# RWKV: output, gate and value products in tiles of 128 tokens, with residual rows brought to the tile and back by DMA

## The chip, the cores and the metric

The kernel runs on one core of a Trainium2 chip (trn2). The metric is device time in microseconds (us). The kernel before takes 3527.89 us, the median of three runs (3525.93 to 3533.52). The kernel after was not run before the prediction went on record.

## What is computed

Four layers work on the same residual stream `x` of 16 sequences, 100 tokens each, 512 channels wide, in fp32 (where the code has `...`, the five mixes of `xa` with its predecessor, the products `r`, `k`, `v`, `w`, `g`, and the normalising of the scan's output `og` per head are left out): a cross-attention block, an RWKV block, a cross-attention block with a feed-forward part, and a second RWKV block. The change is in the RWKV block, which runs twice (layers 1 and 3). Cut to what matters:

```python
def _block(x, state, ...):
    xa = _ln(x, ln1_w, ln1_b)
    ...
    s = a + w_t[..., :, None] * s         # the scan over 100 tokens, a = k_t v_t
    ...
    x1 = x + og * g @ Wo.T                # output product
    xc = _ln(x1, ln2_w, ln2_b)
    sx2 = jnp.concatenate([state[:, 0:1] - xc[:, :1], xc[:, :-1] - xc[:, 1:]], axis=1)
    xk2 = xc + sx2 * ffn_maa_k
    xr2 = xc + sx2 * ffn_maa_r
    rr = jax.nn.sigmoid(xr2 @ Wfr.T)      # gate product
    kk = jnp.square(jax.nn.relu(xk2 @ Wfk.T))   # key product
    return x1 + rr * (kk @ Wfv.T)         # value product
```

The output, gate and value products each multiply 1600 rows by a 512 x 512 matrix. What is added to the residual is one row per token.

## The kernel before

**Layout.** The residual lies in SBUF for the whole kernel as 16 tiles `xb[b]` of 100 tokens by 512 channels, one for each sequence (line 196). RWKV works on groups of `G` = 4 sequences, `T` = 400 tokens. Normalised inputs, the gated scan output (`gc`), the channel part's mixes (`xk`, `xr`) and the squared keys (`kk`) lie turned: 128 channels on partitions, four such pieces for the 512, 400 tokens along the free axis. So the output, gate and value products take 100 columns of such a tile (one sequence) as their left side, the weight's 512 columns as their right side, and sum over the four pieces. `chain` (line 778) records such a product: four matmuls into one PSUM bank, as two halves, each of which is an entry of the queue below, and then `read`.

**The scan and what fills it.** `rwkv` (line 636) is one loop over units `u` (lines 1229 to 1285). The scan has 128 units: 16 chunks (group x 128 channels) of eight. In each unit PE spreads the next values over 128 partitions (`spread`), VectorE does one product and two scans (`product`, `scan`), GpSimd one product with the repeated `r`, and PE gathers sums over two units (`gather`). The rest of the layer lies in the list `pieces`: entries with a cost in us, a first unit (`slot`) and a function. Each unit has a budget `due` (line 1276): 2.5 us up to unit 28, 2.95 up to unit 95, 3.9 after it, less what the unit itself puts on PE. Entries are taken in the order of the list while the budget is positive; a chain that is begun is finished before another. The instructions of PE, VectorE, ScalarE and GpSimd are kept in the order in which the program writes them (lines 65 to 79). SP's queue, on which nearly all loads are issued, is filled by the scheduler of the tile framework: DMAs follow in an order that it derives from the program's order and from when their buffers are ready[...].

**What the list holds.** `projections` (line 799) makes a group's inputs to the scan a group ahead. `output(g)` (line 1210) records the four output products of a group after its last chunk is scanned (at units 32, 64, 96 and 128, to be taken seven units later), ahead of everything else in the list; the residual add on VectorE is put off by one unit with `read_later` (line 183). `channels` (line 971) records the channel part of a group, `channel_stream` (line 1072) strings groups 0 to 2 together (recorded at unit 86, to be taken from unit 93 on), and group 3 is recorded at unit 128. Its parts are: the statistics of `xb` on VectorE, `normed` (ScalarE), `turned` (PE transposes, then ScalarE, GpSimd), the key products `keys` (line 1013), the gate products `gates_of(i)` (line 1026; tanh of the result on ScalarE) and the value products `values(i)` (line 1036; two operations on VectorE, the second of which adds to `xb[b]`). One group's stages are laid around the next group's statistics, in this order (lines 1062 to 1080):

```python
"first":  keys(0..3), gates_of(0), values(0)        # then the next group's statistics
"second": gates_of(1), values(1), gates_of(2), gates_of(3)   # then its normed
"third":  values(2)                                 # then its turned
"fourth": values(3)                                 # then its own first
```

In the last layer `values` also writes the sequence to HBM.

**Buffers.** `stage` gives one of six tiles of 128 x 512 (used by normalised rows, gates and the scan's inputs on their way to HBM); the tag `xm` has three buffers of 128 x 4 x 400, for the mixes; `kk` has one of its own. PSUM has three banks (`mm0` to `mm2`) that all these products share in turn; a bank's late reader is called at the latest when the bank comes round again.

**The scan's own DMAs.** `enter`, `repeat` (line 1099) and `gates` (line 1203) bring a chunk's inputs from HBM on SP's queue: for each half chunk twelve DMAs of 100 KB, which repeat `k`, `w` and `r` over the partitions, and for each chunk four of 200 KB.

Of the kernel before, what the change touches and what calls it, by code (L numbers as in the profile page):

```python
# [9 lines left out]
F32 = mybir.dt.float32  # L10
# [7 lines left out]
G = 4  # L18
# [17 lines left out]
def xattn_sequence(ctx: ExitStack, tc: tile.TileContext, d: dict, out: bass.AP):  # L36
# [599 lines left out]
    def rwkv(n, ws, next_weights, last):  # L636
# [6 lines left out]
        with ExitStack() as es:  # L643
# [83 lines left out]

            steps = lambda t: t.rearrange("p (b t) -> p b t", t=L)
            stage = lambda name: two.tile([128, 512], F32, tag="stage", bufs=6, name=name)
            put = {}  # L730
# [47 lines left out]
            def chain(us, slot, tag, before, ps, lhs, rhs, read):  # L778

                bank = []  # L780

                def half(i):
                    if i == 0:
                        for fn in before:
                            fn()
                        bank.append(slots.bank())
                        begun.append(second)
                    else:
                        begun.clear()
                    for c in (2 * i, 2 * i + 1):  # L790
                        mm(out=ps(bank[0]), lhsT=lhs(c), rhs=rhs(c), start=(c == 0), stop=(c == NC - 1))
                    if i:
                        read(bank[0])

                second = lambda: half(1)
                piece(us / 2, lambda: half(0), slot, tag)
                piece(us / 2, second, slot, tag)

            def projections(g, base):
# [171 lines left out]
            def channels(g, slot):  # L971
# [41 lines left out]
                def keys(co):  # L1013
                    def read(ps):
                        if co == 0:
                            st["kk"] = two.tile([128, NC, T], F32, tag="kk", bufs=1, name=f"kk_{nm}")
                        rl = two.tile([128, T], F32, tag="tm", bufs=4, name=f"rl_{nm}_{co}")
# [8 lines left out]
                def gates_of(i):  # L1026
                    def read(ps):
                        st[i] = stage(f"th_{nm}_{i}")[:L, :]
                        scalar.activation(st[i], ps[:L, :], AF.Tanh, scale=0.5)

                    chain(
                        3.45, slot, None, [], lambda ps: ps[:L, :],
                        lambda c: st["xr"][:, c, i * L : (i + 1) * L], lambda c: cm["Wfr"][:, c, :], read,
                    )

                def values(i):
                    b = g * G + i

                    def read(ps):
                        def add():  # L1040
                            th = st[i]
                            vector.scalar_tensor_tensor(th, th, 1.0, ps[:L, :], ALU.add, ALU.mult)
                            vector.scalar_tensor_tensor(xb[b], th, 0.5, xb[b], ALU.mult, ALU.add)
                            if last:
                                nc.sync.dma_start(out=out[b], in_=xb[b])

                        slots.read_later(ps, add)

                    chain(
                        3.45, slot, None, [], lambda ps: ps[:L, :],  # L1050
                        lambda c: st["kk"][:, c, i * L : (i + 1) * L], lambda c: cm["Wfv"][:, c, :], read,
                    )

                def written(fn):
# [11 lines left out]
                    "first": written(lambda: [keys(co) for co in range(NC)] + [gates_of(0), values(0)]),  # L1066
                    "second": written(lambda: [gates_of(1), values(1), gates_of(2), gates_of(3)]),
                    "third": written(lambda: values(2)),
                    "fourth": written(lambda: values(3)),
# [140 lines left out]
            def output(g, slot):  # L1210

                rest, pieces[:] = pieces[:], []
                before = [lambda: [fn() for c in range(NC) for fn in chunks[NC * g + c]["norm"]]]
                for i in range(G):
                    x = xb[g * G + i]

                    def read(ps, x=x):
                        added[g].append(
                            slots.read_later(ps, lambda: vector.tensor_tensor(x, ps[:L, :], x, ALU.add))
                        )  # L1220

                    chain(
                        3.45, slot, ("wo", g), before, lambda ps: ps[:L, :],
                        lambda c, i=i: chunks[NC * g + c]["g"][:, i * L : (i + 1) * L],
                        lambda c: ws["Wo"][:, c, :], read,
                    )
                pieces.extend(rest)

            UNITS = 32 * NG
            u, due = -42, 0.0  # L1230
            while u < UNITS + 6 or pieces or slots.due:
# [6 lines left out]
                elif u % 32 == 0 and u > 0:  # L1238
                    if u == UNITS:

                        for i in range(len(pieces) - 4, len(pieces)):
                            pieces[i] = (pieces[i][0], u + 8, *pieces[i][2:])
                        rest = channel_stream([NG - 1], u + 8)
                        pieces[len(pieces) - 4 : len(pieces) - 4] = rest[: G + 1]
                        pieces.extend(rest[G + 1 :])
                    output(g - 1, u + 7)
# [28 lines left out]

                due = min(due, 0.0) + (2.5 if 0 <= u < 29 else 2.95 if u < UNITS - 32 else 3.9)
                due -= 0.45 * (u % 2) + 0.7 * (at in (2, 7)) if unit else 0.0
# [444 lines left out]
```

## Time and profile before

| what | us |
|---|---|
| median of three runs | 3527.89 (3525.93 to 3533.52) |
| the profiled execution | 3530.07, of which its span is 3528.3, at a mean granted TensorE clock of 0.935 |
| layer 0 | 0 to 740 |
| RWKV, layer 1: before the scan, scan, after it | 740 to 857, to 1520, to 1600 |
| layer 2: attention, feed-forward | 1600 to 2290, to 2670 |
| RWKV, layer 3: before the scan, scan, after it | 2670 to 2762, to 3430, to 3528 |

The boundaries are rounded, read from the timeline. In the two scans (1331 us together) TensorE is busy for 1245.6 us, VectorE for 885.6 and GpSimd for 811.6. The products that the change touches are these groups of the profile: `mm<-l_Wo,gc` with 256 rows, and for each layer `mm<-l_Wfr,xr` and `mm<-l_Wfv,kk` with 128 rows each, all of 128 x 100 by 128 x 512.

How to read it: PE is TensorE's matmul side, PEld its weight loads, DVE VectorE, ACT ScalarE, POOL GpSimd, SP the sync engine. A row of a group or of the timeline names the engine, the line of the program, the operation, the tile written and the tiles read, their shapes, and how many instructions it stands for; in brackets stands the idle time before it and who ended it. L82 is the helper that records every matmul in program order, and L77 the one for the other engines, so tiles tell operations apart. `SPq` is SP's queue. A layer's number follows the tile's name (`xr_1b`, `kk_3b`).

### The profile page before, as it was taken

What the parts mean: (1) busy time and instruction counts of PE and PEld (TensorE: products, weight loads), DVE (VectorE), ACT (ScalarE), POOL (GpSimd) and SP (SyncE); (2) the same over time, 40 slices, a digit from 0 to 9 for tenths busy, and PEclk for the clock granted to TensorE, in tenths of its full rate; (3) what the DMA queues carried; (4) which work ended last, traced back from release to release, by engine and by line L of the source; (5) the groups of instructions that cost most, each with busy time, mean ns of one, the idle gap of its engine ahead of it and who ended that gap; (6) DMA issues with size and microseconds to landing.
All of it is one profiled execution on the core that took longest, in us unless ns stands there. A gap on an engine that the chain in (4) does not pass through costs nothing. (4 is left out here: it accounts for less than half of the span.)

```text
span 3528.3 us, 46276 instructions
## 1 busy us (share of the span) xinstructions
PE 3217.1 (91%) x17795; PEld 1432.9 (41%) x17795; DVE 1770.8 (50%) x3570; ACT 981.8 (28%) x1715; POOL 1376.4 (39%) x1036
## 2 busy tenths in 40 slices
PE   6899998868999988988999999789998899998898
PEld 3444443333333333334454555345553333333333
DVE  4777777723777665514333333310001477775651
ACT  1322223222233233321322223211112233333232
POOL 1444444443666665511212111210002466665551
PEclk8999999978999989999999999999997899998998
DMA  5000001012434441101000010110012243433310
GB/s 169 21 31 21 31 21 33 1 56 86 126 108 124 126 146 54 38 27 55 25 19 19 19 31 18 39 53 8 10 57 68 87 129 104 134 115 117 87 29 14
DMA packets 153426, 216.60 MB, mean 61 GB/s; under 512 B 23498, under 2 KB 132106, under 8 KB 153206
## 3 DMA queue, kind: packets, MB, share of 16 engines
q1 hardware_dynamic: 130166, 180.87, 17.3%
q10 hardware_dynamic: 23040, 32.78, 2.6%
q8 instruction: 140, 2.29, 0.3%
q14 instruction: 80, 0.66, 0.1%
HBM read 174.25 MB, written 36.04 MB: 60 GB/s over the span
## 5 line engine op out<-in xcount | busy, mean ns | idle before, releaser
L77 POOL TENSOR_TENSOR a<-a,rr 128x800 f32<-128x800 f32 x256 | 480.9, 1879 | 342.4 <-DVE a L77 269.7
L77 DVE TENSOR_TENSOR_SCAN a<-wr,vb 128x400 f32<-128x400 f32 x512 | 475.7, 971 | 19.8 <-PE acc L82 10.9
L77 DVE TENSOR_TENSOR vb<-vb,kr 128x792 f32<-128x792 f32 x256 | 250.5, 979 | 197.0 <-ACT vb L77 195.5
L77 DVE CUSTOM_DVE_ANT_0 junk<-l_sc,mask 100x361 f32<-100x361 f32 x512 | 273.0, 533 | 90.1 <-PE l_sc L82 73.6
L82 PE MATMUL vb<-vc,sel 32*128 32x396 f32 x1024 | 261.0, 568 | 3.4 <-DVE a L77 2.2
L77 DVE TENSOR_TENSOR pt<-l_sc,maskT 121x400 f32<-121x400 f32 x384 | 193.5, 566 | 89.9 <-PE l_sc L82 89.0
L77 ACT ACTIVATE pt<-pt 121x1600 f32<-121x1600 f32 x96 | 147.6, 1538 | 282.2 <-DVE pt L77 280.7
L1425 DVE CUSTOM_DVE_ANT_0 junk<-l2a_sc,mask 100x361 f32<-100x361 f32 x256 | 136.9, 535 | 172.9 <-PE l2a_sc L82 155.7
L77 POOL TENSOR_TENSOR xj<-tm,ext 128x400 f32<-128x400 f32 x160 | 152.8, 962 | 174.3 <-DVE tm L77 168.0
L77 DVE SCALAR_TENSOR_TENSOR tm<-mm,vec,sx 128x400 f32<-128x400 f32 x160 | 99.9, 631 | 235.6 <-PE mm L82 190.9
L1461 POOL TENSOR_TENSOR pa<-pt,pt 121x1600 f32<-121x1600 f32 x16 | 57.2, 3574 | 366.8 <-ACT pt L1456 366.8
L63 PE MATMUL h<-yTb,l_fc 128*128 128x400 f32 x512 | 175.3, 505 | 8.2 <-ACT yTb L229 8.2
L1642 DVE TENSOR_TENSOR x<-pb,x 100x512 f32<-100x512 f32 x16 | 12.8, 799 | 338.3 <-DMA pb<-po 332.7
L82 PE MATMUL v<-l_v_w,ct 128*121 128x512 f32 x384 | 180.0, 613 | 0.0
L82 PE MATMUL k<-ct,l_k_w 128*128 128x361 f32 x512 | 173.0, 481 | 7.3 <-DVE mv_l2a L207 7.3
L77 POOL TENSOR_TENSOR pa<-pt,pt 121x1600 f32<-121x1600 f32 x32 | 114.7, 3586 | 165.5 <-ACT pt L77 165.5
L63 PE MATMUL p<-l_proj,h 128*128 128x512 f32 x384 | 165.4, 592 | 0.0
L77 ACT COPY vb<-s0r 128x8 f32<-128x8 f32 x256 | 43.0, 168 | 408.7 <-PE vb L82 322.9
L82 PE MATMUL l_sc<-kz,qz 32*100 32x361 f32 x1024 | 117.1, 528 | 42.6 <-DVE pt L77 21.7
L82 PEld LDWEIGHTS vb<-vc,sel 32*128 32x128 f32 x1024 | 84.8, 190 | 146.9 <-issue 107.3
L82 PE MATMUL mm<-l_Wo,gc 128*100 128x512 f32 x256 | 124.6, 629 | 8.4 <-POOL gc L77 8.4
L63 PEld LDWEIGHTS h<-yTb,l_fc 128*128 128x128 f32 x512 | 98.1, 192 | 83.3 <-ACT yTb L229 10.1
(258 smaller groups left out, 5305.6 us busy)
## 6 DMA issues: line engine op xcount, KB each, us to landing
kr<-dk SPq DMA_DIRECT2D x256, 100.0 KB
wr<-dw SPq DMA_DIRECT2D x256, 100.0 KB
rr<-dr SPq DMA_DIRECT2D x256, 100.0 KB
ct<-in_ctxT SPq DMA_DIRECT2D x32, 722.0 KB
dk<-k ACTq DMA_DIRECT2D x32, 200.0 KB
kc<-dk SPq DMA_DIRECT2D x32, 200.0 KB
dw<-wd ACTq DMA_DIRECT2D x32, 200.0 KB
dv<-v ACTq DMA_DIRECT2D x32, 200.0 KB
```

The costliest lines, as they stand in the source:

```text
L63: nc.tensor.matmul(out=ps, lhsT=lhs(c), rhs=rhs(c), start=(c == 0), stop=(c == n - 1))
L77: return lambda *args, **kw: tc.keep_in_program_order(op(*args, **kw))
L82: pin(nc.tensor.matmul(**kw))
L1425: nc.vector.tensor_tensor_reduce(out=junk, in0=ss[r][:L, :S2], in1=t["mask"], scale=-1.0, scalar=FLT_MAX, op0=ALU.add, op1=ALU.min, accum_ ...
L1461: nc.gpsimd.tensor_tensor(t["pa"], t["pt"][0], pt, ALU.add)
L1642: nc.vector.tensor_tensor(x, pb[:, i, :], x, ALU.add)
```

## The change

The output, gate and value products no longer go sequence by sequence but in tiles of 128 consecutive tokens of the group: three tiles of 128 and 16 tokens left over. For those 16 the last 32 tokens of the group are taken as the left side, and the 512 output columns are split into four lots of 128, which go into four column groups of 32, so that the result is one 128 x 128 tile: partitions 32r to 32r+31 hold columns 128r to 128r+127 of the last 32 tokens. The first 16 of each 32 are computed twice and not used.

Since a tile of 128 tokens does not match the residual tiles of 100, the residual rows are brought by DMA, SBUF to SBUF, on SP's queue: `rows_in` copies the rows of one or two `xb` tiles into a tile of 128 x 512 (tag `stage`) or, for the left-over, four lots of 32 rows x 128 columns into a tile of the new tag `rest`. VectorE adds there, and `rows_out` copies the rows back. For the output products `rows_in` is issued when the product is begun (`bring`), for the value products when the gate is read. In the last layer the value product's tile goes straight to HBM. Other parts: `kk` takes one of the three `xm` buffers in place of its own; `values(2)` moves from "third" to "second" and `gates_of(3)` from "second" to "third"; the budget is 2.88 in place of 2.95 up to unit 95, 3.5 in place of 3.9 up to unit 127; `output` and the end of the loop are written for either number of entries.

```diff
--- before.py
+++ after.py
@@ -726,6 +726,7 @@
                 scalar.copy(s0r[:, r].rearrange("p c g b -> p (c g b)"), ps[:, : NC * 64])
 
             steps = lambda t: t.rearrange("p (b t) -> p b t", t=L)
+            orow = out.rearrange("b t e -> (b t) e")
             stage = lambda name: two.tile([128, 512], F32, tag="stage", bufs=6, name=name)
             put = {}
             pieces = []
@@ -795,6 +796,59 @@
                 second = lambda: half(1)
                 piece(us / 2, lambda: half(0), slot, tag)
                 piece(us / 2, second, slot, tag)
+            def pieces_of(g, i):
+                for b in range(G):
+                    lo, hi = max(b * L, i * 128), min(b * L + L, i * 128 + 128)
+                    if lo < hi:
+                        rs = slice(lo - b * L, hi - b * L)
+                        yield slice(lo - i * 128, hi - i * 128), xb[g * G + b][rs, :]
+            def rest(g, lo):
+                rs = slice(L - 32 + lo, L)
+                for r in range(4):
+                    ps = slice(32 * r + lo, 32 * r + 32)
+                    yield ps, xb[g * G + G - 1][rs, r * 128 : (r + 1) * 128]
+            def tile_of(nm, i):
+                if i < 3:
+                    return stage(f"{nm}_{i}")
+                return two.tile([128, 128], F32, tag="rest", bufs=3, name=f"{nm}_{i}")
+            def rows_in(nm, g, i):
+                t = tile_of(nm, i)
+                for ps, x in pieces_of(g, i) if i < 3 else rest(g, 0):
+                    nc.sync.dma_start(out=t[ps], in_=x)
+                return t
+            def rows_out(t, g, i):
+                for ps, x in pieces_of(g, i) if i < 3 else rest(g, 16):
+                    nc.sync.dma_start(out=x, in_=t[ps])
+            def row_products(i, slot, tag, before, lhs, rhs, read):
+                if i < 3:
+                    chain(
+                        3.45, slot, tag, before, lambda ps: ps, lambda c: lhs(c)[:, i * 128 : (i + 1) * 128],
+                        rhs, lambda ps: read(ps, ps),
+                    )
+                    return
+                def small():
+                    for fn in before:
+                        fn()
+                    ps = slots.bank()
+                    for c in range(NC):
+                        for r in range(4):
+                            mm(
+                                out=ps[32 * r : 32 * r + 32, :128], lhsT=lhs(c)[:, T - 32 : T],
+                                rhs=rhs(c)[:, r * 128 : (r + 1) * 128], start=(c == 0), stop=(c == NC - 1),
+                            )
+                    read(ps, ps[:, :128])
+                piece(1.0, small, slot, tag)
 
             def projections(g, base):
                 nm = f"{n}_{g}"
@@ -1013,7 +1067,7 @@
                 def keys(co):
                     def read(ps):
                         if co == 0:
-                            st["kk"] = two.tile([128, NC, T], F32, tag="kk", bufs=1, name=f"kk_{nm}")
+                            st["kk"] = two.tile([128, NC, T], F32, tag="xm", bufs=3, name=f"kk_{nm}")
                         rl = two.tile([128, T], F32, tag="tm", bufs=4, name=f"rl_{nm}_{co}")
                         scalar.activation(rl, ps[:, :T], AF.Relu)
                         scalar.activation(st["kk"][:, co, :], rl, AF.Square)
@@ -1024,31 +1078,36 @@
                     )
 
                 def gates_of(i):
-                    def read(ps):
-                        st[i] = stage(f"th_{nm}_{i}")[:L, :]
-                        scalar.activation(st[i], ps[:L, :], AF.Tanh, scale=0.5)
-
-                    chain(
-                        3.45, slot, None, [], lambda ps: ps[:L, :],
-                        lambda c: st["xr"][:, c, i * L : (i + 1) * L], lambda c: cm["Wfr"][:, c, :], read,
+                    def read(ps, got):
+                        st["th", i] = tile_of(f"th_{nm}", i)
+                        scalar.activation(st["th", i], got, AF.Tanh, scale=0.5)
+                        st["x", i] = rows_in(f"cx_{nm}", g, i)
+                    row_products(
+                        i, slot, None, [], lambda c: st["xr"][:, c, :], lambda c: cm["Wfr"][:, c, :], read
                     )
 
                 def values(i):
-                    b = g * G + i
-
-                    def read(ps):
+                    def read(ps, got):
                         def add():
-                            th = st[i]
-                            vector.scalar_tensor_tensor(th, th, 1.0, ps[:L, :], ALU.add, ALU.mult)
-                            vector.scalar_tensor_tensor(xb[b], th, 0.5, xb[b], ALU.mult, ALU.add)
-                            if last:
-                                nc.sync.dma_start(out=out[b], in_=xb[b])
+                            th, x = st["th", i], st["x", i]
+                            vector.scalar_tensor_tensor(th, th, 1.0, got, ALU.add, ALU.mult)
+                            vector.scalar_tensor_tensor(x, th, 0.5, x, ALU.mult, ALU.add)
+                            if not last:
+                                rows_out(x, g, i)
+                            elif i < 3:
+                                nc.sync.dma_start(out=orow[g * T + i * 128 : g * T + (i + 1) * 128], in_=x)
+                            else:
+                                for r in range(4):
+                                    nc.sync.dma_start(
+                                        out=orow[(g + 1) * T - 16 : (g + 1) * T, r * 128 : (r + 1) * 128],
+                                        in_=x[32 * r + 16 : 32 * r + 32],
+                                    )
 
                         slots.read_later(ps, add)
 
-                    chain(
-                        3.45, slot, None, [], lambda ps: ps[:L, :],
-                        lambda c: st["kk"][:, c, i * L : (i + 1) * L], lambda c: cm["Wfv"][:, c, :], read,
+                    row_products(
+                        i, slot, None, [], lambda c: st["kk"][:, c, :], lambda c: cm["Wfv"][:, c, :], read
                     )
 
                 def written(fn):
@@ -1064,8 +1123,8 @@
                     "normed": some(normed, G),
                     "turned": written(lambda: [piece(0.45, lambda c=c: turned(c), slot) for c in range(NC)]),
                     "first": written(lambda: [keys(co) for co in range(NC)] + [gates_of(0), values(0)]),
-                    "second": written(lambda: [gates_of(1), values(1), gates_of(2), gates_of(3)]),
-                    "third": written(lambda: values(2)),
+                    "second": written(lambda: [gates_of(1), values(1), gates_of(2), values(2)]),
+                    "third": written(lambda: gates_of(3)),
                     "fourth": written(lambda: values(3)),
                 }
 
@@ -1209,22 +1268,27 @@
 
             def output(g, slot):
 
-                rest, pieces[:] = pieces[:], []
+                later, pieces[:] = pieces[:], []
                 before = [lambda: [fn() for c in range(NC) for fn in chunks[NC * g + c]["norm"]]]
-                for i in range(G):
-                    x = xb[g * G + i]
-
-                    def read(ps, x=x):
-                        added[g].append(
-                            slots.read_later(ps, lambda: vector.tensor_tensor(x, ps[:L, :], x, ALU.add))
-                        )
-
-                    chain(
-                        3.45, slot, ("wo", g), before, lambda ps: ps[:L, :],
-                        lambda c, i=i: chunks[NC * g + c]["g"][:, i * L : (i + 1) * L],
-                        lambda c: ws["Wo"][:, c, :], read,
-                    )
-                pieces.extend(rest)
+                x = {}
+                def bring(i):
+                    x[i] = rows_in(f"ox_{n}_{g}", g, i)
+                for i in range(4):
+                    def read(ps, got, i=i):
+                        def add():
+                            vector.tensor_tensor(x[i], got, x[i], ALU.add)
+                            rows_out(x[i], g, i)
+                        added[g].append(slots.read_later(ps, add))
+                    row_products(
+                        i, slot, ("wo", g), before + [lambda i=i: bring(i)],
+                        lambda c: chunks[NC * g + c]["g"], lambda c: ws["Wo"][:, c, :], read,
+                    )
+                pieces.extend(later)
 
             UNITS = 32 * NG
             u, due = -42, 0.0
@@ -1238,11 +1302,12 @@
                 elif u % 32 == 0 and u > 0:
                     if u == UNITS:
 
-                        for i in range(len(pieces) - 4, len(pieces)):
+                        kept = max(len(pieces) - 4, 0)
+                        for i in range(kept, len(pieces)):
                             pieces[i] = (pieces[i][0], u + 8, *pieces[i][2:])
-                        rest = channel_stream([NG - 1], u + 8)
-                        pieces[len(pieces) - 4 : len(pieces) - 4] = rest[: G + 1]
-                        pieces.extend(rest[G + 1 :])
+                        own = channel_stream([NG - 1], u + 8)
+                        pieces[kept:kept] = own[: G + 1]
+                        pieces.extend(own[G + 1 :])
                     output(g - 1, u + 7)
                 if u == UNITS - 32 - 3:
                     cm.update(load(n, "Wfk", "Wfr", "Wfv"))
@@ -1273,7 +1338,7 @@
                 if u % 2 and 0 <= (u - 3) // 2 < UNITS // 2:
                     gather((u - 3) // 2)
 
-                due = min(due, 0.0) + (2.5 if 0 <= u < 29 else 2.95 if u < UNITS - 32 else 3.9)
+                due = min(due, 0.0) + (2.5 if 0 <= u < 29 else 2.88 if u < UNITS - 32 else 3.5 if u < UNITS else 3.9)
                 due -= 0.45 * (u % 2) + 0.7 * (at in (2, 7)) if unit else 0.0
                 for p in [p for p in pieces if p[0] == 0 and p[1] <= u]:
                     take(p)
```

## The prediction

> **What bounds the kernel now.** The page's first two parts come first.
>
> ```profile
> span 3528.3 us, 46276 instructions
> PE 3217.1 (91%) x17795; PEld 1432.9 (41%) x17795; DVE 1770.8 (50%) x3570; ACT 981.8 (28%) x1715; POOL 1376.4 (39%) x1036
> ```
>
> TensorE is busy for 91% of the span, VectorE for half. Averages mix stages, so the table by stage comes next (columns: stretch, its length, then busy time of PE, PEld, DVE, ACT, POOL, granted clock, DMA share, GB/s). The first three rows are the scan of layer 1, the fourth its tail.
>
> ```profile
> 857.00:1012.00 155.00, 148.38 (x544) 56.75 (x542) 113.38 (x140) 48.73 (x105) 107.47 (x89) 0.89 0.37 110
> 1012.00:1330.00 318.00, 298.15 (x1140) 113.69 (x1141) 222.19 (x276) 105.98 (x219) 206.04 (x167) 0.93 0.41 122
> 1330.00:1520.00 190.00, 177.76 (x591) 64.14 (x590) 105.84 (x129) 63.85 (x122) 91.72 (x74) 0.94 0.15 43
> 1520.00:1606.00 86.00, 68.11 (x162) 27.93 (x161) 20.70 (x41) 19.98 (x33) 16.90 (x24) 0.87 0.20 66
> ```
>
> In the scan PE is busy 94 to 96% of the time and DVE 56 to 73%. Work taken from PE there is worth nearly its length. What one matmul costs stands in the timeline (start, length, engine, operation):
>
> ```profile
> 1576.40 3.60 PE L82 MATMUL mm<-l_Wfr,xr_1b 128*100 128x512 f32 x8
> 1579.83 3.60 PE L82 MATMUL mm<-l_Wfv,kk_1b 128*100 128x512 f32 x8
> ...
> 2392.18 3.70 PE L1629 MATMUL p<-l_proj,h 128*32 128x128 f32 x128
> 2395.81 1.59 PE L226 MATMUL lnT_l2b<-ident,xn_l2b 100*128 100x100 f32 x16
> ```
>
> The trace has two rows for each fp32 matmul. A chain of four at 512 columns (8 rows) starts 3.43 us before the next. The 592 ns that the groups give for one row is its latency, not its price; the price is 0.43 us. The third line is the same shape of work as the new small piece, in layer 2: 64 matmuls over four column groups take 3.63 us, or 0.057 us each.
>
> [...] four small ones of layer 2 land about 1.9 us after the last issue begins:
>
> ```profile
> 2664.56 2.75 SPq L1636 DMA_DIRECT2D pb<-pr  x4
> ...
> 2668.54 0.69 DVE L1642 TENSOR_TENSOR x<-pb,x 100x512 f32<-100x512 f32 x1 [1.20 <-DMA pb<-pr]
> ```
>
> [...] after the 4.22 us wait below, weight loads stand 0.86 us apart instead of 0.43 for 6 us.
>
> **The change, part by part.**
>
> (a) PE. Each product of a group had four chains, 4 x 3.43. It now has three, and 16 small matmuls: 16 x 0.057 = 0.91. It saves 3.43 - 0.91 = 2.52 us. The layer-2 rows 128*128 128x512 keep the 0.43 us interval, so 128 rows of output cost no more than 100. There are 3 products x 4 groups x 2 layers = 24: 60.5 us at full clock. How much is realised? I set the built order of both kernels out unit by unit (a unit is one product and two scans), with 0.43 and 0.335 us a row for 512 and 400 columns, and DVE at 0.98, 0.93 and 0.58 to 0.69 us. Per layer PE loses 6.4 us in units 29 to 95, 13.0 in 96 to 125, 10.9 in the tail. The sum over units of the larger of PE and DVE falls by 4.8, 10.7 and 10.9: 26.4, or 52.8 for both layers. PE runs ahead of DVE across units, so the truth lies between 52.8 and 60.5: I take 57. The new pacing (2.88 for 2.95, 3.5 for 3.9) leaves each unit's place in the order nearly as it was; it is in this sum.
>
> (b) DVE and ACT do three reads of 128x512 and one of 128x128 for four of 100x512. The reads (0.69 us) do not grow with partitions; the fourth shrinks. 0.45 us each, three adds a product pair, is some 10 us over the kernel, on engines with slack: nothing.
>
> (c) SP issues 10 copies in and 10 out for each output product and each pair of gate and value products (7 out in the last layer's pair): 308 copies, 16 old ones gone. At 0.43 us an issue that is about 125 us on a queue that is idle for most of 3528. Bytes: about 24 MB more, beside 217. Throughput costs nothing; order does. Rows out wait for DVE's add and hold all that SP has behind them, the scan's repeats above all. In the built order those repeats then stand three to four units (14 to 18 us) ahead of need, and take about 9 (twelve issued from 1032.07 on had landed by 1041.44): nothing. Rows in: most tiles have two units (9 us) or more. The exception is the small output tile of groups 0 and 1 (units 45 and 77): it stands behind the tile before it going out, and seven repeats: 0.9 + 3.0 to 4.2 + 1.7 issue + 1.9 landing = 7.5 to 8.7 us, after 4.5 us of a unit. DVE stalls 3 to 4 us; its slack ahead of PE's next spread is about 2 us. 1.5 us x 4 places = 6 us (0 to 12).
>
> (d) Order in the channel part. Before, a whole value chain (3.43) stood between one group's turned rows and the next group's keys; now a small one (0.91). The keys wait for POOL already:
>
> ```profile
> 1395.39 3.29 POOL L77 TENSOR_TENSOR sx_1b<-ext_1b 128x400 f32<-128x400 f32 x4
> ...
> 1401.08 0.94 PE L82 MATMUL mm<-xk_1b,l_Wfk 128*128 128x400 f32 x2 [2.96 <-POOL xk_1b L77]
> ...
> 1475.16 0.94 PE L82 MATMUL mm<-xk_1b,l_Wfk 128*128 128x400 f32 x2 [1.70 <-POOL xk_1b L77]
> ```
>
> The POOL chain is unchanged, so 2.5 us of cover is lost at two groups in each layer: 10 us[...]: 12 (4 to 20).
>
> (e) Tail. The last output product now goes through a copy before its statistics:
>
> ```profile
> 3451.05 14.45 PE L82 MATMUL mm<-l_Wo,gc 128*100 128x512 f32 x26 [4.22 <-POOL gc L77]
> ...
> 3465.34 7.03 PE L82 MATMUL mm<-l_Wfv,kk_3b 128*100 128x512 f32 x16
> ...
> 3471.52 2.93 ACT L77 ACTIVATE xn_3b<-x,shift_3b,rstd_3b 100x512 f32<-100x512 f32 x4 [21.62 <-POOL shift_3b L77]
> ...
> 3472.38 0.30 PE L85 MATMUL mm<-ident,xn_3b 100*128 100x100 f32 x1
> ```
>
> From the end of Wo to the first transpose 7.0 us pass, just hidden by two value chains. Afterwards: add 0.5, four issues 1.7, landing 1.9, one bn_stats and aggregate 0.9, POOL 2.0, ACT 0.8: 7.8 us, covered by one chain and two small ones, 5.2. 2.6 us x 2 layers = 5, and 1 for the clock: 6 (2 to 10).
>
> (f) From layer 1 to 2, layer 2's first context load waits until rwkv's tiles are free (issued at 1598.83, 0.15 us after the last add). Now it waits for the last rows out: +3.6, and the shorter adds give back 0.9: 3 (1 to 5). At the kernel's end the same adds help: -1.
>
> (g) `kk` shares the three `xm` buffers; in the built order each one's last reader on PE precedes its next writer: nothing, unless POOL's mix of the gate input comes early (then in d).
>
> Sum: -57 + 6 + 12 + 6 + 3 - 1 = -31 us. The profiled execution took 3530.07 us, its span plus 1.8; the median is 2.2 lower. 3527.9 - 31 = 3497.
>
> **Rivals.** *Waits cost nothing in the scan* (all 60.5 realised, only e and f left, 9): 3476. For it: PE's 94 to 96%; against it: the POOL wait in d is in the profile. *Gain eaten*: d and e at double, c at its upper end (12 + 40 - 1 + 5 = 56 against 57): about 3527. [...] *Slower, by the rows' round trip*: some 42 row tiles come in during the two scans, on a DMA that is 40% busy. If each stalls DVE by more than its 2 us of slack, PE's spread waits with it. Beyond 31/42 = 0.75 us of PE time a tile the change loses; with rows 5 us behind the repeats (seven of 100 KB, at the 1200 KB in 9.4 us of those twelve, are 5.5 us) half of them would lose 2.5: 42 x 1.2 = 50, less the 31: 3547. Against it: the built order gives most tiles two units. [...]
>
> **Chances.** Forecast 0.60 (own range 3483 to 3512); cheap waits 0.24; gain eaten 0.07; slower 0.09. The range 3473 to 3518 leaves out the slower case, the eaten one and the best end of the cheap one. About 0.2% (7 us) is what a measurement of this kernel can tell from no change: faster by more 0.86, within 0.05, slower 0.09.
>
> **What would show it.** Wo, Wfr and Wfv at 192 rows each over both layers instead of 256, with the small shape beside them; PE's busy time down by about 55; new DVE waits for `ox` of 1 to 4 us at four places; keys waiting 5 us instead of 3 for POOL; a gap of 2 to 3 us before the tail's transposes; the first layer-2 keys 3 us later after the last value product. Wrong: DVE waits for `ox` or `cx` of over 40 us in all, or repeats landing late for POOL.

## The result and the profile after

The changed kernel takes 3519.09 us (median of 8 runs, 3510.95 to 3523.93) against 3529.43 for the kernel before in the same comparison: a ratio of 0.9966, with a 95% interval of 0.9954 to 0.9978. That is 12 us less (8 to 16); forecast were 31, and the range ended at 3518. The profiled execution took 3521.39 us, its span 3519.3. Below, "against before" is always a kernel's ratio to runs of before on the same chip, less 1, times 3528; the 95% intervals reach 3 to 7 us to each side, so a difference between two kernels is good to some 5 to 9 us.

The head of the page after:

```profile
span 3519.3 us, 47909 instructions
PE 3191.7 (91%) x18371; PEld 1448.5 (41%) x18371; DVE 1759.3 (50%) x3570; ACT 978.0 (28%) x1715; POOL 1374.2 (39%) x1036
```

PE's busy time fell by 25.4 us, where 55 were expected. Yet the products are what was forecast. Two groups of matmuls of the kernel after (count, busy us, mean ns, idle time before them):

```profile
L82 PE MATMUL mm<-l_Wo,gc 128*128 128x512 f32 x192 | 96.0, 640 | 8.4 <-POOL gc L77 8.4
...
L82 PE MATMUL mm<-l_Wo,gc 128*32 128x128 f32 x256 | 8.6, 276 | 0.0
```

192 rows in place of 256, and eight small pieces in 8.6 us, 1.1 each. So the work is gone and something else keeps PE "busy". The table by stage shows what: stretches from scan unit to scan unit, first of the kernel before (layer 1: units 29 to 95; units 96 to 126; unit 127 and the tail, up to layer 2's first key matmul; then unit 127 and the tail of layer 3), then of the kernel after. The columns are those of the prediction's table; the number before the last two is the mean granted clock.

```profile
987.25:1313.26 326.01, 302.35 (x1153) 115.39 (x1154) 227.77 (x284) 112.18 (x229) 216.95 (x179) 0.92 0.42 125
1313.26:1499.38 186.12, 173.88 (x593) 63.25 (x593) 110.45 (x133) 64.68 (x127) 98.30 (x79) 0.93 0.18 51
1499.38:1605.80 106.42, 88.53 (x222) 35.27 (x220) 26.02 (x48) 23.57 (x38) 18.77 (x25) 0.89 0.16 53
...
3424.52:3528.30 103.78, 88.88 (x218) 35.03 (x216) 19.53 (x31) 23.58 (x38) 16.44 (x20) 0.90 0.06 16
```

```profile
987.82:1324.81 336.99, 314.10 (x1197) 120.91 (x1198) 227.16 (x284) 107.62 (x222) 210.15 (x172) 0.89 0.43 130
1324.81:1505.32 180.51, 164.16 (x713) 64.96 (x713) 107.83 (x133) 67.42 (x134) 102.88 (x86) 0.92 0.29 85
1505.32:1611.77 106.45, 79.41 (x346) 37.20 (x344) 22.04 (x42) 23.80 (x39) 20.04 (x26) 0.86 0.29 93
...
3423.43:3519.30 95.87, 79.22 (x342) 36.93 (x340) 17.68 (x31) 23.81 (x39) 18.04 (x21) 0.89 0.16 49
```

Units 29 to 95 are 11 us longer, with less to do: PE is busy 12 us more, at a clock of 0.89 in place of 0.92. At half clock the same pair of matmuls is busy for 1.70 us in place of 0.94 (both are shown below), so busy time is not work. The tail has 9 us less of PE time and the same length: 27.0 us without PE in place of 17.9. So three quantities are kept apart from here on, in the profiled execution of each kernel, summed over both RWKV layers from unit 0 to the end of the tail: gaps (length less PE's busy time), the loss to half clock (half of the busy time inside the spells for which the trace's clock records show half the clock), and the work that is left.

| kernel | against before, us | length | gaps | half-clock loss | work |
|---|---|---|---|---|---|
| before | 0 | 1489.9 | 110.0 | 94.1 | 1285.9 |
| e9: before, late budget 3.5 | -37 | 1452.4 | 85.7 | 81.7 | 1284.9 |
| e5: before, both new budgets | -30 | 1463.3 | 79.0 | 87.2 | 1297.1 |
| e11: before, 2.88 and 3.1 | -45 | 1442.7 | 73.4 | 75.1 | 1294.3 |
| e13: changed, old budgets | +8 | 1499.7 | 146.3 | 114.7 | 1238.7 |
| changed | -12 | 1486.9 | 127.0 | 123.8 | 1236.1 |
| e3: output products alone | -13 | 1476.4 | 98.9 | 102.7 | 1274.9 |
| e4: gate and value products alone | -28 | 1465.4 | 108.1 | 99.3 | 1258.1 |
| e2: changed, own rows | -37 | 1450.4 | 116.9 | 95.9 | 1237.7 |
| e7: e2 and a chain as cover | -62 | 1440.6 | 102.7 | 99.8 | 1238.1 |
| e10: e7 with 3.1 | -83 | 1414.0 | 90.6 | 86.4 | 1236.9 |
| e12: e10 with 2.95 | -48 | 1441.2 | 103.9 | 100.6 | 1236.7 |

Work is good to about 12 us: the four kernels with the products of before give 1285 to 1297. The loss to half clock is good to about 7 us a layer: before and e9 run the same program up to unit 95 of each layer, and units 29 to 95 of layer 3 took 325.9 us in one and 332.5 in the other, with gaps of 23.4 and 23.6 and a half-clock loss of 19.0 and 25.9. The profiled executions lie up to 7 us from their kernel's median, so lengths need not differ as the first column does.

Against e5, which has its budgets, the changed kernel has 61.0 us less work, as forecast, and 48.0 us more gaps and 36.6 more half clock.

### The profile page after: what moved, and what is told of

Its sections match the earlier page's. It is cut to its first block, busy times and chain, and to the rows that moved or that the text cites. A ratio compares the mean times of both kernels' runs of the same rounds, so it can differ in the third digit from the quotient of the medians.

```text
span 3519.3 us, 47909 instructions
## 1 busy us (share of the span) xinstructions
PE 3191.7 (91%) x18371; PEld 1448.5 (41%) x18371; DVE 1759.3 (50%) x3570; ACT 978.0 (28%) x1715; POOL 1374.2 (39%) x1036
## 3 DMA queue, kind: packets, MB, share of 16 engines
q1 hardware_dynamic: 148106, 204.35, 19.4%
## 5 line engine op out<-in xcount | busy, mean ns | idle before, releaser
L77 POOL TENSOR_TENSOR pa<-pt,pt 121x1600 f32<-121x1600 f32 x32 | 114.7, 3583 | 165.2 <-ACT pt L77 165.2
L77 POOL TENSOR_TENSOR pa<-pa,pt 119x1600 f32<-119x1600 f32 x32 | 114.4, 3575 | 42.5 <-ACT pt L77 42.3
```

The lines of the kernel that those rows point to most:

```text
L77: return lambda *args, **kw: tc.keep_in_program_order(op(*args, **kw))
```

## The experiments

The theory after the result (A): the left-over output tile stalls VectorE and PE at four places, and half clock follows. Rivals: the gain was lost ahead of the keys (B), or on SP's queue as such (C). This is the place at unit 45 in the kernel after (start, length, engine; SPq is SP's queue):

```profile
1058.24 0.69 DVE L77 TENSOR_TENSOR ox<-mm,ox 128x512 f32<-128x512 f32 x1 [1.85 <-PE mm L82]
...
1058.95 1.66 SPq L828 DMA_DIRECT2D x<-ox  x2
...
1060.65 1.48 SPq L1164 DMA_DIRECT2D wr<-dw  x3
1062.25 1.77 SPq L1164 DMA_DIRECT2D rr<-dr  x4
...
1064.06 2.49 SPq L823 DMA_DIRECT2D ox<-x  x4
...
1067.82 0.29 DVE L77 TENSOR_TENSOR ox<-mm,ox 128x128 f32<-128x128 f32 x1 [6.24 <-DMA ox<-x]
...
1068.26 0.91 PE L82 MATMUL mm<-tz,td_maa_w 64*128 64x400 f32 x2 [2.81 <-DVE ox L77]
...
1078.55 1.70 PE L82 MATMUL mm<-tz,td_maa_w 64*128 64x400 f32 x2
```

SP's queue issues nothing from 1057.48 to 1058.95, until the third tile's add has ended (1058.93). Then the third tile goes out, the seven repeats behind it follow, and the left-over tile comes in, 8.9 us after the third tile's add. VectorE waits 6.2 us, PE 2.8 for a PSUM bank, and then a pair of matmuls takes 1.70 in place of 0.9 us: by the clock records PE is at half clock for 20.5 us here; before, for 6.8.

**e1, the left-over tile first.**

```diff
 def bring(i):
-    x[i] = rows_in(f"ox_{n}_{g}", g, i)
+    for k in {0: (3, 0), 3: ()}.get(i, (i,)):
+        x[k] = rows_in(f"ox_{n}_{g}", g, k)
```

> One edit: the left-over tile's residual rows of each output product are brought when the first tile is begun, before the third tile's rows go back. Theory A (the loss is the round trip of the left-over output tile in groups 0 and 1: VectorE waits 6.3 us at four places, PE then stalls about 3 us and runs some 10 to 14 us longer at half clock, about 9 us a place, 36 in all): VectorE's waits for ox fall from 25 us to under 3, the half-clock spells after units 45 and 77 shrink from 17-20 us to 7, and the time falls by 28 to 36 us, to 3483 to 3491. Theory B (the gain of the small matmuls was never there, or is lost to the key and transpose waits): within 8 us of the changed kernel, 3511 to 3519. Theory C (SP's queue is loaded as such, and the repeats come late): the waits move to other tiles, little is gained, 3505 to 3519.

Measured: 3490.34 us, ratio 0.9898 (0.9882 to 0.9914), 36 us against before and 24 less than the changed kernel. VectorE's waits for ox fell from 25.1 us to none. A holds, B and C fall for this part.

**e2, own rows.** `lots` are three fixed tiles, set to zero once; the sums in the partitions for which no rows are brought are not used.

```diff
-for ps, x in pieces_of(g, i) if i < 3 else rest(g, 0):
+for ps, x in pieces_of(g, i) if i < 3 else rest(g, 16):
...
-return two.tile([128, 128], F32, tag="rest", bufs=3, name=f"{nm}_{i}")
+return next(lots)
```

> One edit: for the left-over tile only the 16 rows that it owns are brought, not the 32 that it computes, so that its way in no longer depends on the third tile's way out; the other partitions hold zeros from the start, and their sums are not used. The order of the program is unchanged. Theory A, if the dependency alone sets the place on the queue: the same as with the tile brought first, 3483 to 3491. If instead the number of copies on the queue counts, as many as before are issued: 3511 to 3519, unchanged.

Measured: 3488.01, ratio 0.9895 (0.9880 to 0.9909). The same as e1 (3490.34), with as many copies as in the changed kernel, and 25 us less than it: the dependency sets the place, not the number of copies. The left-over add now comes early, at unit 45:

```profile
1055.46 0.28 DVE L77 TENSOR_TENSOR rest<-mm,rest 128x128 f32<-128x128 f32 x1
...
1059.34 0.94 PE L82 MATMUL mm<-tz,td_maa_w 64*128 64x400 f32 x2
```

In units 29 to 95 the changed kernel has 5.7 us more gaps and 12.2 more half-clock loss than e2 in layer 1, and 5.3 and 7.2 in layer 3: 11.0 and 19.4 in both. Against e1 it is 11.4 and 14.3. So in both comparisons the half clock costs more than the stall itself.

**e3 and e4, one half of the tiling each.**

```diff
# e3: gates_of, values and their order as before
-row_products(i, slot, None, [], lambda c: st["xr"][:, c, :], lambda c: cm["Wfr"][:, c, :], read)
+chain(3.45, slot, None, [], lambda ps: ps[:L, :], lambda c: st["xr"][:, c, i * L : (i + 1) * L], ...)
# e4: output as before
-row_products(i, slot, ("wo", g), before + [lambda i=i: bring(i)], ...)
+chain(3.45, slot, ("wo", g), before, lambda ps: ps[:L, :], ...)
```

> Only the output products in tiles of 128; gate and value products, and their order, as before; kk in the mixes' buffers and the new budgets stay. Theory A: 8 of the 24 products save 20 us, the four stalls cost 36, the tails 5: slower than before by about 15 to 20 us, 3545. Theory B (loss in the channel part: lost cover ahead of keys): faster than before by 12 to 15, 3515.

> Only the gate and value products in tiles of 128, with their new order, buffers and budgets; the output products as before. Theory A: 16 products save 40 us, the key waits cost some 10, the boundary to layer 2 some 5: faster than before by about 25, 3504. Theory B (the cover lost ahead of the keys eats the gain): within 8 us of before, 3521 to 3529.

Measured: e3 3515.90, ratio 0.9963 (0.9950 to 0.9975); e4 3501.81, ratio 0.9922 (0.9908 to 0.9935). e4 came out where A had it and e3 where B had it, and together they would be 41 us faster where the changed kernel is 12. Neither theory had a place for that, so the question was what both share with the changed kernel: the budgets.

**e5, the budgets alone.**

```diff
-due = min(due, 0.0) + (2.5 if 0 <= u < 29 else 2.95 if u < UNITS - 32 else 3.9)
+due = min(due, 0.0) + (2.5 if 0 <= u < 29 else 2.88 if u < UNITS - 32 else 3.5 if u < UNITS else 3.9)
```

> The kernel before with the new budgets alone (2.88 and 3.5 us a unit). The prediction has them at nothing: 3523 to 3531. Rival: with only the output products tiled, units 96 to 127 got 17 to 19 us shorter in each layer, though one output product lies there; if the budget of 3.5 does that, those units shorten here by 10 or more as well, and what is left over lengthens the tails: 3510 to 3522 if part of it stays.

Measured: 3501.78, ratio 0.9916 (0.9904 to 0.9929), 30 us faster than before, without one tile of 128. So e4's tiles are worth nothing (3501.81 beside 3501.78), e3's cost 17, and the changed kernel's cost 18: A's hit on e4 was chance, and its forecast of e3, 18 slower, holds once e5 is the base. What the budget does shows in units 96 to 126 and in unit 127 with the tail, in layer 1 of e5:

```profile
1310.73:1476.57 165.84, 158.93 (x560) 56.16 (x559) 109.64 (x133) 64.38 (x126) 97.96 (x80) 0.96 0.22 60
1476.57:1591.25 114.68, 100.06 (x257) 41.55 (x258) 26.48 (x49) 28.10 (x47) 26.17 (x32) 0.93 0.15 49
```

The units are 20 us shorter, the tail only 8 longer. With fewer pieces a unit, PE no longer reaches the keys before GpSimd's mixes: the waits of 2.96 and 1.70 us for `xk` and of 4.09 for `rk` are gone, and one of 1.35 for `xk` is left. And the tail has products left to put under its own waits. This is the same e5, ahead of the last output product, where the kernel before waited 4.22 us for `gc`:

```profile
1499.11 1.88 PE L82 MATMUL mm<-l_Wfr,xr_1b 128*100 128x512 f32 x4
1500.83 3.60 PE L82 MATMUL mm<-l_Wfv,kk_1b 128*100 128x512 f32 x8
1504.26 7.03 PE L82 MATMUL mm<-l_Wfr,xr_1b 128*100 128x512 f32 x16
1511.13 13.90 PE L82 MATMUL mm<-l_Wo,gc 128*100 128x512 f32 x32
```

**e6 and e13, the old budgets** in e2 and in the changed kernel (the reverse of e5's diff).

> The left-over tile brings only its own rows, as in e2, and the budgets are those of before. If the budgets are worth nothing: 3484 to 3492, as e2. If the lower budgets carried part of the gain: 3495 or more; if they cost (units 29 to 95 of the channel-only kernel were 3.4 us longer in each layer than before): 3478 to 3483.

> The changed kernel with the budgets of before, nothing else undone: the fourth corner beside before (3527), before with the new budgets (3502) and the changed kernel (3519). If the tiles' loss does not depend on the budget (17 us at the new ones): 3540 to 3550. If the tiles need the lower budget, as own rows did (50 us between the old and the new budgets): 3560 to 3575. The prediction's own step, budgets worth nothing: 3515 to 3523.

Measured: e6 3538.46, ratio 1.0024 (1.0013 to 1.0034); e13 3536.01, ratio 1.0023 (1.0014 to 1.0032). The tiles cost 8 us at the old budgets and 18 at the new ones; the budgets give 30 without tiles and 20 with them. All three guesses for e13 were off, and e6 went far beyond its "3495 or more". Own rows gain nothing at the old budgets (e6 and e13 are equal), because the stall of theory A is not there in e13. At unit 44 the left-over add follows the third tile's at once:

```profile
1056.58 0.69 DVE L77 TENSOR_TENSOR ox<-mm,ox 128x512 f32<-128x512 f32 x1 [1.85 <-PE mm L82]
1057.62 0.29 DVE L77 TENSOR_TENSOR ox<-mm,ox 128x128 f32<-128x128 f32 x1 [0.35 <-PE mm L82]
```

Its rows come in there from 744.6 us on, ahead of the scan, and the third tile's rows go out from 1057.29 on; in the changed kernel the left-over rows come in last (1064.06 after 1058.95, shown above). At the other three places the gap is 0.35 us as well. VectorE does wait 16.1 us for ox in e13, but for three other tiles, those of the third group (units 104 to 107). So the stall belongs to the budget of 2.88 as well as to the dependency.

**e7 and e8, a whole chain as cover ahead of the keys**, e8 with the old budgets.

```diff
-"second": written(lambda: [gates_of(1), values(1), gates_of(2), values(2)]),
-"third": written(lambda: gates_of(3)),
-"fourth": written(lambda: values(3)),
+"second": written(lambda: [gates_of(1), values(1), gates_of(2), gates_of(3)]),
+"third": written(lambda: values(3)),
+"fourth": written(lambda: values(2)),
```

> As e2, and the order in the channel part is gates 1, values 1, gates 2, gates 3, then the small value product, then the next group's transposes, then the value product of the third tile: a whole chain of 3.43 us stands again between the transposes and the keys, where a small one of 0.9 stood. Prediction's step d (2.5 us of cover at two groups in each layer, and some half clock): the key waits fall from 5.3 and 3.9 us back to about 3.0 and 1.7, and 8 to 12 us are gained on e2's 3488: 3476 to 3480. Rival: the wait only moves to the next one for GpSimd (the wait for rk of 4 us that stood there before comes back): 3484 to 3490.

> As e7, with the budgets of before. If both effects are what e6 and e7 show by themselves, they add up: e7's time plus the difference of e6 from e2. If budgets and order work on the same waits, it stands within 4 us of the better one of the two.

Measured: e7 3468.78, ratio 0.9824 (0.9811 to 0.9837), 25 us less than e2 (18 to 32 by the intervals); e8 3512.99, ratio 0.9945 (0.9931 to 0.9959), 28 less than e6. In the changed kernel and in e7 the first of these key waits is:

```profile
1418.75 1.70 PE L82 MATMUL mm<-xk_1b,l_Wfk 128*128 128x400 f32 x2 [5.29 <-POOL xk_1b L77]
...
1482.00 1.63 PE L82 MATMUL mm<-xk_1b,l_Wfk 128*128 128x400 f32 x2 [3.86 <-POOL xk_1b L77]
```

```profile
1389.33 0.94 PE L82 MATMUL mm<-xk_1b,l_Wfk 128*128 128x400 f32 x2 [1.59 <-POOL xk_1b L77]
```

The second wait in e7 is under 1.4 us; in layer 1 of e2, from which e7 starts, PE waits 2.29, 0.53 and 4.53 us at the first of the two and 3.85 at the second. The 4 us wait for `rk` did not come back: layer 1 has a new one of 1.93, layer 3 none. The gain is twice step d's 12, and it adds to the budgets' (25 and 28). Not all of it is cover. The order of e7 also ends the layer with a tile of 128, two copies out, in place of the left-over one, four, and PE waits less ahead of layer 2 (e2, then e7):

```profile
1587.99 0.76 PE L85 MATMUL m8T<-ident,mfr 16*121 16x16 f32 x3 [14.29 <-DMA m<-in_mask]
```

```profile
1576.17 0.75 PE L85 MATMUL m8T<-ident,mfr 16*121 16x16 f32 x3 [9.68 <-DVE mfr L1572]
```

In the profiles units 96 to 126 of the two layers, where the key waits lie, are 15.3 us shorter in e7 than in e2.

**e14, the old order of entries alone** in the changed kernel ("second": gates 1, values 1, gates 2, gates 3; "third": values 2; "fourth": values 3).

> The changed kernel with the order of entries of before: gates 3 ahead of the next group's normed rows, the whole chain of value product 2 ahead of the transposes, the small value product after them. The keys still have only a small product as cover, so step d says nothing changes there: 3515 to 3523. If the move of gates 3 behind the normed rows is what delays GpSimd's mixes: 3500 to 3512.

Measured: 3520.11, ratio 0.9980 (0.9972 to 0.9988), 7 us against before and 5 from the changed kernel; the two intervals overlap. As d says: the small piece, not the moved entries, is what leaves the keys bare.

**e9, e10, e11, e12, one budget each.** 3.5 late with 2.95 early (e9); e7 with 2.88 and 3.1 (e10); before with 2.88 and 3.1 (e11); e10 with 2.95 early (e12). The edits are shown against the line with both new budgets.

```diff
# e10, e11
-3.5 if u < UNITS else 3.9
+3.1 if u < UNITS else 3.9
# e9, e12
-2.88 if u < UNITS - 32
+2.95 if u < UNITS - 32
```

> The kernel before with the later of the two budgets alone: 3.5 us a unit from unit 96 to 127, and 2.95 kept ahead of it. Both budgets together gave 3502. If the later one does it (it removes the key waits of 3.0 and 1.7, the rk wait of 4.1 and the gc wait of 4.2 us from the profile): 3500 to 3510. If the earlier one does (the units before 29 were 4 us shorter in each layer): 3518 to 3527.

> As e7, with 3.1 in place of 3.5 us a unit from unit 96 to 127. Theory D (a budget that is too large for what is left in the list drains the channel part ahead of GpSimd and ScalarE, and leaves the tail no work to put under its waits; tiles take work out of the list, so the budget has to fall with it): the gc wait of 4.2 us at the head of each tail goes, the gaps of units 96 to 127 fall from 12 to under 8 us, and 8 to 18 us are gained: 3451 to 3461. Rival: 3.5 happens to suit one order of pieces, and the waits only move: 3463 to 3478.

> The kernel before with 2.88, and 3.1 us a unit from unit 96 to 127. At 3.5 the profile shows no key wait and no gc wait that a still lower budget could take away, so theory D gives little: 3496 to 3506, within 5 us of the 3502 at 3.5. If a lower budget is good by itself, whatever is in the list: 3485 to 3494.

> As e10, with the earlier budget of before, 2.95 in place of 2.88. In the kernel before, 2.88 cost 12 us (3502 with both new budgets, 3490 with the later one alone), though units 0 to 28 got 4 us shorter in each layer. If that cost belongs to the budget: 3428 to 3436. If it belongs to where that kernel's pieces happen to fall: 3440 to 3452.

Measured: e9 3489.80, ratio 0.9895 (0.9878 to 0.9911); e10 3443.24, 0.9766 (0.9747 to 0.9786); e11 3480.78, 0.9872 (0.9855 to 0.9889); e12 3477.59, 0.9865 (0.9845 to 0.9885). The later budget does it all: 37 us alone. e10 is 83 us faster than before, faster than both kernels of this case. The gc waits at the head of its two tails are gone; in layer 1 products stand there (e10, then the changed kernel's tail in layer 3):

```profile
1489.71 3.60 PE L82 MATMUL mm<-l_Wfv,kk_1b 128*128 128x512 f32 x8
1493.14 3.60 PE L82 MATMUL mm<-l_Wfr,xr_1b 128*128 128x512 f32 x8
1496.58 11.47 PE L82 MATMUL mm<-l_Wo,gc 128*128 128x512 f32 x56
```

```profile
3441.35 2.74 PE L82 MATMUL mm<-l_Wo,gc 128*128 128x512 f32 x6
3448.31 10.62 PE L82 MATMUL mm<-l_Wo,gc 128*128 128x512 f32 x50 [4.22 <-POOL gc L77]
```

Theory D (the budget must fall with the list) is right on the gc wait, and the gain was larger than forecast (20 us on e7); but the gaps of units 96 to 126 fell only from 12.3 and 11.6 us to 10.9 and 8.6, not under 8. And e11 limits it: the kernel before gains another 15 us over e5 from 3.1 as well, in half clock above all (87.2 to 75.1), so a lower budget is good in itself here. With 3.1 the tiles, with own rows and the cover, are at last worth 37 us (e10 against e11). e12 contradicts both its guesses: 2.95 costs 35 us in e10, where in the kernel before it gained 7, about as much as the intervals can tell. The waits ahead of unit 96 do not explain this, since they go with the early budget in both kernels. Here is the one for normed rows in e12 and e9, which have 2.95, then in e10 and e5, which have 2.88:

```profile
1302.52 0.43 PE L85 MATMUL mm<-ident,xn_1b 100*128 100x100 f32 x1 [8.19 <-ACT xn_1b L77]
...
1298.66 0.43 PE L85 MATMUL mm<-ident,xn_1b 100*128 100x100 f32 x1 [8.19 <-ACT xn_1b L77]
```

```profile
1300.80 0.43 PE L85 MATMUL mm<-ident,xn_1b 100*128 100x100 f32 x1 [6.37 <-ACT xn_1b L77]
...
1304.25 0.43 PE L85 MATMUL mm<-ident,xn_1b 100*128 100x100 f32 x1 [6.38 <-ACT xn_1b L77]
```

In both pairs 2.95 adds 14 us of gaps in units 29 to 95 of the two layers. In the kernel before the later stretches make up for it (e9 against e5: 7 us fewer gaps after unit 95, 5.5 less half clock, and 12 less work, which is as far as work is good to); in e12 they do not, and half clock grows by 14.2 as well. Why is not settled.

## Why the prediction was wrong

The direction was right by luck; the size was 12 instead of 31, by two errors of opposite sign and a premise behind both. The tiles and what comes with them cost 18 us (changed kernel against e5), where the prediction had them gain 31; the new budgets, which it had at nothing, gave 30 (e5 against before). The tiles take 60.5 us of work away and still cost 18, so some 79 us were lost, where the prediction allowed 29.5.

- **The premise, "work taken from PE there is worth nearly its length".** It rested on PE's busy share of 94 to 96% in the scan. That share holds half-clock time: 94.1 of 1489.9 us are lost to it before. The sentence on the unit-by-unit sum, with full-clock prices and PE or VectorE as the larger, had no term for either gaps or clock. The work of step a is gone as forecast (61.0 against e5, forecast 60.5 at full clock, of which 57 were to show); it came back as gaps and half clock.
- **Step a, "the new pacing ... leaves each unit's place in the order nearly as it was; it is in this sum".** Wrong, and the largest single term: the budgets alone gave 30 us (e5). I judged places by unit, while what counts is how far the list is drained when GpSimd's mixes are due and when the tail begins.
- **Step c, the left-over output tile, 6 us.** The place and the chain were right. The cost was 25 (e2), for two reasons: VectorE's wait was 6.2 us, not 3 to 4, because only 2.7 us of its unit's work stood between the adds (two scans and a product, 1058.85 to 1061.58), not 4.5; and the half clock after the stall was left out, 19.4 of the 29.2 us that the two layers' units 29 to 95 differ by (14.3 of 24.2 against e1). The number of copies is not the cause: e2 has as many and takes 25 us less. What copies cost in throughput was not measured by itself. The stall also needs the budget of 2.88 (e13), which the step did not see.
- **Step d, 12 us.** The wait came as written, 5 us in place of 3. Giving the cover back gained 25 in all, of which about 5 lie at the boundary to layer 2 and belong to step f. In units 96 to 126 gaps sank by 9.4 us and half clock by 6.5 in e7 against e2. Right mechanism, a cost of about 15 to 20; the half clock, put at 2 by the author's estimate, was mis-sized.
- **Step e, 6 us.** The gap ahead of the tail's transposes was put at 2 to 3 us; the profile after has 3.87 and 3.55. It was costed as the only loss of the tail. Its other one, the 4.22 us wait for `gc`, was there before, and the new budgets alone would have covered it; tiles leave too little in the list to do so.
- **Step f, 3 us.** It was 6.7. The first context load of layer 2 is issued at 1607.42, behind the last rows out, and the keys wait 14.0 us where they waited 7.3 (kernel after; last line: kernel before):

```profile
1602.72 3.39 SPq L828 DMA_DIRECT2D x<-cx_1b  x5
1607.42 0.37 SPq L1389 DMA_DIRECT2D ct<-in_ctxT  x1
...
1611.77 1.54 PE L82 MATMUL k<-ct,l_k_w 128*128 128x361 f32 x2 [13.98 <-DMA ct<-in_ctxT]
```

```profile
1605.80 1.54 PE L82 MATMUL k<-ct,l_k_w 128*128 128x361 f32 x2 [7.30 <-DVE mv_l2a L207]
```

- **Step b and step g** were not tried by themselves. e4 has their edits for the channel part and equals e5, with 39.0 us less work: that its gain is lost does not show which step took it.
- **The rivals.** "Gain eaten" was nearest in kind, but I gave it 0.07 and had c in it at 12, half its size. Its sum also has a slip: d and e at double are 36, not 40, which makes 3523 and not 3527. "Slower, by the rows' round trip" named the right place and too many tiles: one tile of four stalls.

What stays open: of the 79 us that the tiles lost, e2 and e7 give back 50 (c, and d with a part of f). How the other 28 or so divide is not settled. The profiles show where they lie: e7 has 23.7 us more gaps than e5, 13.9 of them in the tails and 10.1 in units 96 to 126, and 12.6 more half-clock loss.

## What to carry to other kernels

Before pricing work that is taken from an engine at nearly full share, split its busy time into work, half clock and gaps, and see whether the work to be removed is what covers somebody's wait. Where an order is laid out by costs and budgets, a change to a budget is a change of its own: test it alone, on the kernel before, ahead of everything else. When two halves of a change do not add up, look for what both halves share.

## What the runs showed of the hardware

Half clock came after short idle times. In the kernel after PE waited 2.8 us at unit 45 and then ran at half clock for 20.5. In the kernel before a spell of 6.8 us begins at 1071.3; the only idle time of PE in the 10 us ahead of it is one of 0.59, which ended at 1067.81. One of 10.2 us begins at 1146.4, within a wait of 1.75 (1146.16 to 1147.91) that has 1.08 us of idle time in the 10 us ahead of it. Step d's 2 us for half clock rested on longer idling ahead of the keys; that was the author's estimate, and these two spells came without it. The clock records list 49 spells of half clock before and 53 after; in each profile all but the one that ends with the program last 3.41 us or a multiple of it, up to 27.3. Over both RWKV layers the loss was 94.1 us of 1489.9 before (6.3%) and 123.8 of 1486.9 after (8.3%); the difference, 29.7 us, is nearly the whole gain that was forecast. What sets the length of a spell was not tried; it is not the program alone, since the same units 29 to 95 lost 19.0 us in one execution and 25.9 in another (before and e9, layer 3).

The small pieces over four column groups cost about what step a has for them. The one at unit 45 starts 1.01 us ahead of the next matmul (1058.99 and 1060.00), where 0.91 was forecast. Layer 0 of the kernel before has matmuls of 128 columns that are not spread over column groups (`v<-l_wv,ct`): 12 of them, 24 rows from 57.91 on, take 2.88 us, 0.24 each, against 0.057 each for the 64 of L1629.
